# A graph network on one core: the last gathers in two buffers, output between their batches, float16 scale factors behind the output projection

## The chip, the cores and the metric

The kernel runs on one core of a Trainium2 chip. The metric is the device time of one execution in microseconds (us); the time before is the median of five runs. A profiled execution gives a trace with the time of every instruction on each engine: PE (matrix products; PEld its weight loads), DVE (vector), ACT (scalar functions), POOL (GpSimd, which here also issues the indirect DMAs) and SP (which issues the other DMAs).

## The reference

Four layers over a graph of N = 3327 nodes with 128 features and a dense 0/1 adjacency matrix `adj`. Every layer computes `x = x + layer(relu(layernorm(x)), adj)`.

```
layer 0   two rounds of swish((adj @ h) @ W + b)
layer 1   attention in 128 heads of width 8, scores + 2 * adj, softmax, then out @ Wo.T
layer 2   agg = adj @ h; msg = relu(agg @ W_msg.T + b); GRU cell of msg and h
layer 3   lap(A, x) = d * (A @ (d * x)),  d = 1 / sqrt(row sums of A)
          z = leaky_relu(lap(adj, h) @ W1 + b1)
          S = exp(-distance(z_i, z_j) / 2), only the 4 nearest of each row kept
          out = lap(S + adj, h) @ W2 + b2
```

In the last line the product with `S + adj` falls into two parts: a dense product with `adj`, and a sum over four rows per node, weighted by S. One of the four is the node itself.

## The kernel before

Nodes are laid out as 128 partitions by T = 26 tiles. Layer 0 and the projections take some 0.6 ms, the attention runs from there to about 10610 us by an order written out by hand, and everything that follows is the function `tail(general)`. There a scheduler decides at build time in which order the instructions of each engine stand; at run time each engine works through its own list in order, and semaphores connect them. `tail(False)` is what runs here; `tail(True)` is a general version in a loop that is passed zero times.

`tail` begins with the output projection of the attention (pool `lo`). For each of the 26 tiles, a load brings `o` (SP, L664), DVE normalises it (L666, L667), PE transposes it (L672), ACT copies the transposes to `oT` (L673), PE multiplies by `wo_s` into `yp` (L676) and DVE adds `yp` to `xs` (L677). Three buffers hold `o`. Pieces of tiles (0 to 3, 4 to 12, 13 to 25) go through the LayerNorm (L157 to L164) as soon as they are ready, and are split into two float16 parts (L214, L218) for the products with `adj`. The second product (L230, 26 loads of a 16-bit row block by L227) and layer 2 follow, then the layer 3 product, the distances with the four largest entries of each row (L862, L863), and the last product.

Ahead of the projection in the source stands `scales` (L586 to L625). It works out, from the largest and smallest `d1` and the norms of the columns of `w2`, the scale factors with which values are brought into float16 range: `d1_in`, `d1_out`, `into4`, `back4` and the flag `wide`. It has one small matrix product on PE (L601, into `c2`), which needs the square of `w2_s` (ACT, L598), two reductions of it (DVE, L602, L603), a square root (ACT, L605), a maximum over partitions (POOL, L595) and some dozen DVE instructions on 1 to 26 columns (L606 to L624). `d1_in` is first used behind layer 2.

Rows `y` of all nodes are written to DRAM (`yd`). While the last dense product runs, `gather(t)` collects the neighbours: for each tile of a batch three indirect DMAs on POOL (L886, 128 rows of 512 bytes each) fill `rows`; DVE multiplies by `sim` (L895, reading `rows`), adds up (L896, L897), scales (L898) and adds to `xs` (L899). L894 begins the sum of the next batch with the node's own row. There are five batches of 5, 5, 5, 5 and 6 tiles, and one buffer `rows`, so the gathers of a batch wait until L895 of the batch before has read it. When the product is done, seven PSUM accumulators are copied to `agg`, four of them by DVE (L191), three by ACT (L189). Then the output: in groups of four tiles PE transposes `agg` (L908), DVE scales it (L910) and adds `xs` (L911), and SP writes `o` to `out` with three DMAs (L914). The pool of `o` has three buffers.

Of the kernel before, what the change touches and what calls it, by code (L numbers as in the profile page):

```python
# [8 lines left out]
F32 = mybir.dt.float32  # L9
# [9 lines left out]
PSUM = bass.MemoryType.PSUM  # L19
DRAM = bass.MemoryType.DRAM  # L20

P = 128
# [23 lines left out]
def quads():  # L46
    return [(a, min(4, T - a)) for a in range(0, T, 4)]
# [7 lines left out]
def kernel(  # L55
# [65 lines left out]
    def over_t(small, t0=0, n=T):  # L121
        return small[:, t0 : t0 + n].unsqueeze(2).to_broadcast([P, n, D])
# [5 lines left out]
    def inv_sqrt(pool, src, name, scale=1.0, bias=0.0):  # L128
        r = pool.tile([P, T], F32, name=name)
        nc.scalar.activation(r, src, AF.Sqrt, bias=bias, scale=scale)  # L130
        nc.vector.reciprocal(r, r)
        return r
# [453 lines left out]
    def scales(pool, d1):  # L586

        d1_in, d1_out = (pool.tile([P, T], F32, name=name) for name in ("d1_in", "d1_out"))
        into4, back4 = (pool.tile([P, 1], F32, name=name) for name in ("into4", "back4"))

        ends = pool.tile([P, 4], F32, name="ends")
        both = pool.tile([P, 2], F32, name="both")
        nc.vector.tensor_reduce(both[:, 0:1], d1, AX.X, ALU.max)
        nc.vector.tensor_reduce(both[:, 1:2], d1, AX.X, ALU.min, negate=True)
        nc.gpsimd.partition_all_reduce(ends[:, :2], both, P, bass_isa.ReduceOp.max)  # L595
        sq = pool.tile([P, P + D], F32, name="w2_sq")
        nc.vector.memset(sq[:, :P], 1.0)
        nc.scalar.activation(sq[:, P:], w2_s, AF.Square)  # L598
        with tc.tile_pool(name="sc_ps", bufs=1, space=PSUM) as ps:
            c2 = ps.tile([P, D], F32, name="c2")  # L600
            nc.tensor.matmul(c2, sq[:, :P], sq[:, P:], start=True, stop=True)  # L601
            nc.vector.tensor_reduce(ends[:, 2:3], c2, AX.X, ALU.max)  # L602
            nc.vector.tensor_reduce(ends[:, 3:4], c2, AX.X, ALU.min, negate=True)  # L603
        top = pool.tile([P, 2], F32, name="ends_top")
        nc.scalar.activation(top[:, 1:2], ends[:, 2:3], AF.Sqrt, bias=tiny_c)  # L605
        nc.vector.tensor_copy(top[:, 0:1], ends[:, 0:1])  # L606
        low = pool.tile([P, 2], F32, name="ends_low")

        nc.vector.tensor_scalar(low[:, 0:1], ends[:, 1:2], -(2.0**5), None, op0=ALU.mult)
        nc.vector.tensor_scalar(low[:, 1:2], ends[:, 3:4], -(2.0**12), None, op0=ALU.mult)  # L610
        fit = pool.tile([P, 2], F32, name="ends_fit")
        nc.vector.tensor_tensor(fit[:, 0:1], ends[:, 0:1], low[:, 0:1], op=ALU.is_le)
        nc.vector.tensor_tensor(fit[:, 1:2], ends[:, 2:3], low[:, 1:2], op=ALU.is_le)
        nc.vector.tensor_mul(wide, fit[:, 0:1], fit[:, 1:2])
        nc.vector.tensor_scalar(wide, wide, -1.0, 1.0, op0=ALU.mult, op1=ALU.add)

        inv = pool.tile([P, 2], F32, name="ends_inv")
        nc.vector.reciprocal(inv, top)
        nc.vector.tensor_mul(into4, inv[:, 0:1], inv[:, 1:2])
        nc.vector.tensor_mul(back4, top[:, 0:1], top[:, 1:2])  # L620
        nc.vector.tensor_scalar(d1_in, d1, inv[:, 0:1], PART, op0=ALU.mult, op1=ALU.mult)
        nc.vector.tensor_scalar(d1_out, d1, top[:, 0:1], 0.5 / PART, op0=ALU.mult, op1=ALU.mult)
        nc.vector.tensor_scalar_mul(into4, into4, PART / 2)
        nc.vector.tensor_scalar_mul(back4, back4, 1.0 / PART)  # L624
        return d1_in, d1_out, into4, back4  # L625
# [4 lines left out]
    def tail(general):  # L630
# [13 lines left out]
        with ExitStack() as s:  # L644
# [4 lines left out]
                split_unless_general(parts, h, p, scale=PART)  # L649

            h, done = layernorm_relu(pool, halved)
            d1 = inv_sqrt(pool, deg, "d1")
            d1_in, d1_out = d1, d1
            if not general:
                d1_in, d1_out, into4, back4 = scales(pool, d1)
            with tc.tile_pool(name="lo", bufs=3) as lo, tc.tile_pool(name="lo_ps", bufs=2, space=PSUM) as ps:
                wo_s = lo.tile([NH, E, D], F32, name="wo_s", bufs=1)
                nc.gpsimd.dma_start(wo_s, wo)
                for t in range(T):
                    kp = rows_of(t)  # L660
                    o = lo.tile([P, EA, NH], F32, name="o")
                    src = ot.rearrange("e (p t c) -> t p e c", t=T, c=NH)[t]
                    for p0, p1 in ((0, kp),) if kp == P else ((0, 112), (112, kp)):
                        nc.sync.dma_start(o[p0:p1], src[p0:p1])  # L664
                    inv = lo.tile([P, NH], F32, name="inv")
                    nc.vector.reciprocal(inv[:kp], o[:kp, E, :])  # L666
                    nc.vector.tensor_mul(o[:kp, :E, :], o[:kp, :E, :], inv[:kp].unsqueeze(1).to_broadcast([kp, E, NH]))  # L667
                    oT = lo.tile([NH, E, P], F32, name="oT")
                    for quad in range(2):
                        tp = ps.tile([P, 4, P], F32, name="tp")  # L670
                        for j in range(4):
                            nc.tensor.transpose(tp[:, j, :kp], o[:kp, 4 * quad + j, :], ident[:kp, :kp])  # L672
                        nc.scalar.copy(oT[:, 4 * quad : 4 * quad + 4, :kp], tp[:, :, :kp])  # L673
                    yp = ps.tile([P, D], F32, name="yp")
                    for e in range(E):
                        nc.tensor.matmul(yp[:kp], oT[:, e, :kp], wo_s[:, e, :], start=(e == 0), stop=(e == E - 1))  # L676
                    nc.vector.tensor_add(xs[:kp, t, :], xs[:kp, t, :], yp[:kp])  # L677
                    done(t + 1)


            a_pool = s.enter_context(tc.tile_pool(name="adj_in", bufs=1 if general else 4))
# [190 lines left out]
                nc.vector.tensor_sub(moved[:, T - 1 :], moved[:, T - 1 :], last_row)  # L872


            cuts = list(range(0, T - T % 5, 5)) + [T]
            near_0 = 0 if general else 1

            def gather(t):
                if t not in cuts[:-1]:
                    return  # L880
                p = slice(t, cuts[cuts.index(t) + 1])
                n = p.stop - p.start
                rows = gpool.tile([P, n, 4 - near_0, D], F32, name="rows")
                for i in range(n):
                    for k in range(near_0, 4):
                        nc.gpsimd.indirect_dma_start(  # L886
                            out=rows[:, i, k - near_0, :],
                            out_offset=None,
                            in_=yd,
                            in_offset=bass.IndirectOffsetOnAxis(ap=idx[:, t + i, k : k + 1], axis=0),  # L890
                        )
                w = gpool.tile([P, n, 4, D], F32, name="w")
                if not general:
                    nc.vector.tensor_mul(w[:, :, 0], y[:, p], sim[:, p, 0:1].to_broadcast([P, n, D]))  # L894
                nc.vector.tensor_mul(w[:, :, near_0:], rows, sim[:, p, near_0:].unsqueeze(3).to_broadcast([P, n, 4 - near_0, D]))  # L895
                nc.vector.tensor_add(w[:, :, 0:2], w[:, :, 0:2], w[:, :, 2:4])  # L896
                nc.vector.tensor_add(w[:, :, 0], w[:, :, 0], w[:, :, 1])  # L897
                nc.vector.tensor_mul(w[:, :, 0], w[:, :, 0], over_t(d2_out, t, n))  # L898
                nc.vector.tensor_add(xs[:, p], xs[:, p], w[:, :, 0])  # L899

            with tc.tile_pool(name="l3_g", bufs=1) as gpool:
                agg = new_agg(pool)
                adj_product(agg, y, parts, gather)
            with tc.tile_pool(name="l3_o", bufs=3) as opool, tc.tile_pool(name="l3_ops", bufs=3, space=PSUM) as ps:
                for t0, n in quads():
                    op = ps.tile([P, 4, D], F32, name="op")
                    for j in range(n):
                        nc.tensor.transpose(op[:, j, :], slots(agg)[:, t0 + j, :], ident)  # L908
                    o = opool.tile([P, 4, D], F32, name="o")
                    nc.vector.tensor_mul(o[:, :n], op[:, :n], over_t(d2_out, t0, n))  # L910
                    nc.vector.tensor_add(o[:, :n], o[:, :n], xs[:, t0 : t0 + n, :])  # L911
                    for p0, p1, n_t in ROW_PARTS:
                        m = min(t0 + n, n_t) - t0
                        nc.sync.dma_start(dram(out, (p0 * T + t0) * D, [[T * D, p1 - p0], [D, m], [1, D]]), o[p0:p1, :m])  # L914
            if not general:
                need = pool.tile([P, 1], F32, name="need")
                nc.vector.tensor_reduce(need, moved, AX.X, ALU.max)
# [130 lines left out]
```

## Time and profile before

| | us |
|---|---|
| median of 5 runs | 11358.35 |
| lowest and highest run | 11336.96, 11369.28 |
| the profiled execution | 11340.12 |
| its span, first to last instruction | 11338.3 |

| stretch of the profile (us) | what runs |
|---|---|
| 600 to 10610 | projections and attention |
| 10611 to 10715 | output projection; PE busy 80 of 104 us |
| 10715 to 11181.7 | layers 2 and 3 up to the first gather |
| 11181.7 to 11303 | gathers; POOL busy 82.4 of 121.3 us |
| 11303 to 11338.3 | last batch, output, end of the program |

Over the whole span PE is busy 96% of the time, ACT 90%, DVE 83% and POOL 50%; these shares are those of the attention and say little about the two short stretches that the change touches. In the profile, a row gives an instruction's start and length in us; the brackets give how long its engine had been idle before it, and what ended that.

### The profile page before, as it was taken

How to read it: one execution, taken by the hardware profiler on the slowest of the kernel's cores; microseconds unless marked ns; L12 is line 12 of the kernel's file. 1: busy time of each engine (PE TensorE's matmuls, PEld its weight loads, DVE VectorE, ACT ScalarE, POOL GpSimd, SP SyncE). 2: the span in 40 equal slices, each digit the busy share in tenths (PEclk: the TensorE clock that was granted, in tenths of full speed). 3: DMA queues.
4: the chain of work that ended last, by engine and by line, in shares of the span. 5: the costliest groups of instructions: out<-in, count | busy, mean ns of one | idle time of the engine just before them, and what ended most of it. 6: DMA issues, size and time to landing. Idle time of an engine off the chain costs nothing. (4 is left out here: it accounts for less than half of the span.)

```text
span 11338.3 us, 210656 instructions
## 1 busy us (share of the span) xinstructions
PE 10935.1 (96%) x79505; PEld 3034.8 (27%) x79530; DVE 9415.2 (83%) x15475; ACT 10223.5 (90%) x9152; POOL 5711.6 (50%) x6196
## 2 busy tenths in 40 slices
PE   9789999999999999999999999999999999999896
PEld 4322222222222222222222222222222222222453
DVE  8678888888888888888888888888888888888655
ACT  0379999999999999999999999999999999999532
POOL 0135555555555555555555555555555555555203
PEclk9899999999999999999999999999999999999998
DMA  7754444444444444444444444444444443444432
GB/s 265 243 126 62 65 67 61 65 66 61 69 63 63 68 62 67 65 61 68 63 65 68 61 65 66 60 68 64 61 69 61 64 63 54 60 57 57 139 106 96
DMA packets 475903, 888.06 MB, mean 78 GB/s; under 512 B 91473, under 2 KB 422722, under 8 KB 439293
## 3 DMA queue, kind: packets, MB, share of 16 engines
q1 hardware_dynamic: 471114, 864.70, 43.7%
q8 instruction: 629, 10.31, 0.5%
q0 software_dynamic: 3760, 9.79, 0.3%
q14 instruction: 400, 3.27, 0.1%
HBM read 761.66 MB, written 112.46 MB: 77 GB/s over the span
## 5 line engine op out<-in xcount | busy, mean ns | idle before, releaser
L497 DVE TENSOR_TENSOR p<-early,a 128x476 f32<-128x476 f32 (+1 forms) x14560 | 8441.4, 646 | 1428.7 <-PE early L492 1178.5
L502 ACT ACTIVATE p<-p 128x2380 f32<-128x2380 f32 (+1 forms) x2912 | 6742.7, 2315 | 15.8 <-DVE p L497 0.4
L509 PE MATMUL acc<-p,v 128*9 128x476 f32 (+1 forms) x46592 | 5887.7, 564 | 44.6 <-POOL p L500 24.6
L500 POOL TENSOR_TENSOR p<-p,e 128x476 f32<-128x476 f32 (+1 forms) x2912 | 3538.8, 1215 | 3286.2 <-ACT p L498 3227.1
L498 ACT ACTIVATE p<-late 128x476 f32<-128x476 f32 (+1 forms) x5824 | 4513.4, 892 | 49.4 <-PE late L495 27.8
L492 PE MATMUL early<-q,k 32*128 32x476 f32 (+1 forms) x14560 | 2882.6, 477 | 18.6 <-DVE p L497 18.6
L492 PE MATMUL late<-q,k 32*128 32x476 f32 (+1 forms) x8736 | 2798.1, 478 | 62.0 <-ACT p L498 36.3
L374 POOL CAST k<-k_in 128x256 fp32r<-128x256 f32 x2912 | 1944.7, 701 | 1185.5 <-DMA q<-qt 577.0
L492 PEld LDWEIGHTS late<-q,k 32*128 32x128 f32 x8736 | 1065.4, 181 | 4765.5 <-ACT p L498 3197.4
L495 PE MATMUL late<-a,two_i 128*128 128x476 bf16 (+1 forms) x5824 | 2180.8, 374 | 0.0
L492 PEld LDWEIGHTS early<-q,k 32*128 32x128 f32 x14560 | 1144.2, 181 | 23.2 <-DVE p L497 19.3
L509 PEld LDWEIGHTS acc<-p,v 128*9 128x9 f32 x46592 | 711.4, 88 | 1424.7 <-issue 1184.5
L495 PEld LDWEIGHTS <-two_i 128*128 128x128 bf16 x5824 | 556.1, 95 | 1328.5 <-issue 1328.5
L189 ACT COPY agg<-agg_ps 128x512 f32<-128x512 f32 x15 | 8.2, 591 | 489.5 <-PE agg_ps L204 289.8
L230 PE MATMUL agg_ps<-a,part 128*128 128x512 bf16 (+1 forms) x1067 | 227.8, 370 | 8.9 <-ACT agg L861 3.2
L272 POOL TENSOR_SCALAR a<-a_in 128x476 bf16<-128x476 f32 (+2 forms) x156 | 222.0, 1423 | 0.5
L410 ACT ACTIVATE qk_st<-pp 128x1024 fp32r<-128x1024 f32 (+1 forms) x52 | 53.3, 1024 | 148.5 <-DMA qt<-qk_st 69.7
L856 PE MATMUL sp<-yT,hT 128*128 128x512 f32 (+1 forms) x364 | 170.9, 611 | 12.3 <-ACT agg L861 6.3
L272 POOL TENSOR_SCALAR a<-a 128x476 bf16<-128x476 f32 (+1 forms) x26 | 36.4, 1402 | 287.2 <-DMA a<-in_adjT_dram 287.2
L204 PE MATMUL agg_ps<-a,h 128*128 128x512 f32 (+2 forms) x364 | 147.5, 568 | 26.7 <-DVE h L164 26.7
L411 DVE SCALAR_TENSOR_TENSOR qk_st<-pp,qk_st 128x1024 fp32r<-128x1024 f32 (+1 forms) x52 | 63.7, 1224 | 122.3 <-ACT qk_st L410 122.3
L518 DVE COPY o<-acc 105x476 f32<-105x476 f32 (+1 forms) x224 | 144.4, 645 | 4.6 <-PE acc L509 4.6
(231 smaller groups left out, 2427.5 us busy)
## 6 DMA issues: line engine op xcount, KB each, us to landing
k_in<-kt SPq DMA_DIRECT2D x1792, 208.0 KB
v<-vd SPq DMA_DIRECT2D x896, 117.0 KB
a<-in_adjT_dram SPq DMA_DIRECT2D x50, 1663.5 KB
a<-adj SPq DMA_DIRECT2D x78, 831.8 KB
q<-qt SPq DMA_DIRECT2D x3072, 14.9 KB
a_in<-in_adjT_dram SPq DMA_DIRECT2D x125, 238.0 KB
qt<-qk_st SPq DMA_DIRECT2D x25, 1024.0 KB
kt<-qk_st SPq DMA_DIRECT2D x25, 1024.0 KB
```

The source lines that it names most:

```text
L204: nc.tensor.matmul(acc[c][:, :w], lhs[:kp, t, :], a[:kp, c0 : c0 + w], start=(t == 0), stop=(t == T - 1))
L230: nc.tensor.matmul(acc[c][:, :w], part[:, t, :], a[:, c0 : c0 + w], start=(t == 0 and i == 0), stop=(t == T - 1 and i == len(parts) - 1),)
L272: nc.gpsimd.tensor_scalar(a2[:kp, :w], a, 2.0, None, op0=ALU.mult)
L374: nc.gpsimd.tensor_copy(k, slots(k_in)[:, t : t + 2, :])
L492: nc.tensor.matmul(sp[:, :we], pairs[t // 2][r, t % 2, :], q4[r, :we], start=True, stop=ways[i] != "I")
L495: nc.tensor.matmul(late[:, i - n_d, :we], two_i, a2[:, :we], start=False, stop=True)
L497: nc.vector.tensor_tensor(p8[:, places[i], :we], early[i][:, :we], a2[:, :we], op=ALU.add)
L498: nc.scalar.activation(p8[:, places[n_d] : places[3] + 1, :we], late[:, :, :we], AF.Exp)
L500: nc.gpsimd.tensor_tensor(p8[:, places[3], :we], p8[:, places[3], :we], e_a[:, :we], op=ALU.mult)
L502: nc.scalar.activation(p8[:, :5, :we], p8[:, :5, :we], AF.Exp)
L509: nc.tensor.matmul(acc[32 * i : 32 * i + EA, :w], v4[:kp, i, t, :], p8[:kp, PLACES[t % 2][i], :w], start=(t == 0), stop=(t == T - 1),)
L856: nc.tensor.matmul(sp[:, c0 : c0 + w], slots(zT)[:, t, :], z2T[:, cols], start=True, stop=False)
```

## The change

Three edits, all in `tail`:

- `inv_sqrt` and `scales`, with all they compute, move in the source from ahead of the output projection to behind it.
- The last gathers are cut into six batches of 5, 5, 5, 5, 4 and 2 tiles, in two buffers: batches 0, 1, 2 and 4 use `rows0`, batches 3 and 5 use `rows1`.
- Only batches 0, 1 and 2 are given to the product as work beside it. The other three follow in the source, and the groups of the output that are complete are written between them.

Line numbers of the changed kernel: the projection is L660 (load), L662, L663, L668, L669, L672, L673; the gathers are L888, the sums L896 to L901; the output is L916 (transposes), L918, L919 and L922.

```diff
             h, done = layernorm_relu(pool, halved)
-            d1 = inv_sqrt(pool, deg, "d1")
-            d1_in, d1_out = d1, d1
-            if not general:
-                d1_in, d1_out, into4, back4 = scales(pool, d1)
             with tc.tile_pool(name="lo", bufs=3) as lo, tc.tile_pool(name="lo_ps", bufs=2, space=PSUM) as ps:
...
                     done(t + 1)
+
+            d1 = inv_sqrt(pool, deg, "d1")
+            d1_in, d1_out = d1, d1
+            if not general:
+                d1_in, d1_out, into4, back4 = scales(pool, d1)
...
-            cuts = list(range(0, T - T % 5, 5)) + [T]
+            cuts = [c for c in (0, 5, 10, 15, 20, 24) if c < T] + [T]
             near_0 = 0 if general else 1
-
-            def gather(t):
-                if t not in cuts[:-1]:
-                    return
-                p = slice(t, cuts[cuts.index(t) + 1])
+            batches = [slice(t0, t1) for t0, t1 in zip(cuts, cuts[1:])]
+
+            def gather(i):
+                p = batches[i]
                 n = p.stop - p.start
-                rows = gpool.tile([P, n, 4 - near_0, D], F32, name="rows")
+                turn = i % 2 if i > 2 else 0
+                rows = gpool.tile([P, n, 4 - near_0, D], F32, name=f"rows{turn}")
...
+            n_beside = min(3, len(batches))
             with tc.tile_pool(name="l3_g", bufs=1) as gpool:
                 agg = new_agg(pool)
-                adj_product(agg, y, parts, gather)
-            with tc.tile_pool(name="l3_o", bufs=3) as opool, tc.tile_pool(name="l3_ops", bufs=3, space=PSUM) as ps:
-                for t0, n in quads():
+                adj_product(agg, y, parts, lambda t: gather(cuts.index(t)) if t in cuts[:n_beside] else None)
+                with tc.tile_pool(name="l3_o", bufs=3) as opool, tc.tile_pool(name="l3_ops", bufs=3, space=PSUM) as ps:
+                    to_write = quads()
+                    for i in range(n_beside - 1, len(batches)):
+                        if i >= n_beside:
+                            gather(i)
+                        while to_write and sum(to_write[0]) <= batches[i].stop:
+                            t0, n = to_write.pop(0)
...
```

The body that writes one group of the output is the same as before, indented further.

More of the change, by code (lines that the diff above doesn't have):

```diff
@@ L872, in tail @@
                 nc.vector.tensor_sub(moved[:, T - 1 :], moved[:, T - 1 :], last_row)
-            cuts = list(range(0, T - T % 5, 5)) + [T]
+            cuts = [c for c in (0, 5, 10, 15, 20, 24) if c < T] + [T]
             near_0 = 0 if general else 1
-            def gather(t):
-                if t not in cuts[:-1]:
-                    return
-                p = slice(t, cuts[cuts.index(t) + 1])
+            batches = [slice(t0, t1) for t0, t1 in zip(cuts, cuts[1:])]
+            def gather(i):
+                p = batches[i]
                 n = p.stop - p.start
-                rows = gpool.tile([P, n, 4 - near_0, D], F32, name="rows")
-                for i in range(n):
+                turn = i % 2 if i > 2 else 0
+                rows = gpool.tile([P, n, 4 - near_0, D], F32, name=f"rows{turn}")
+                for j in range(n):
                     for k in range(near_0, 4):
                         nc.gpsimd.indirect_dma_start(
-                            out=rows[:, i, k - near_0, :],
+                            out=rows[:, j, k - near_0, :],
                             out_offset=None,
                             in_=yd,
-                            in_offset=bass.IndirectOffsetOnAxis(ap=idx[:, t + i, k : k + 1], axis=0),
+                            in_offset=bass.IndirectOffsetOnAxis(ap=idx[:, p.start + j, k : k + 1], axis=0),
                         )
@@ L897, in gather @@
                 nc.vector.tensor_add(w[:, :, 0], w[:, :, 0], w[:, :, 1])
-                nc.vector.tensor_mul(w[:, :, 0], w[:, :, 0], over_t(d2_out, t, n))
+                nc.vector.tensor_mul(w[:, :, 0], w[:, :, 0], over_t(d2_out, p.start, n))
                 nc.vector.tensor_add(xs[:, p], xs[:, p], w[:, :, 0])
+            n_beside = min(3, len(batches))
             with tc.tile_pool(name="l3_g", bufs=1) as gpool:
                 agg = new_agg(pool)
-                adj_product(agg, y, parts, gather)
@@ L904, in tail @@
-            with tc.tile_pool(name="l3_o", bufs=3) as opool, tc.tile_pool(name="l3_ops", bufs=3, space=PSUM) as ps:
-                for t0, n in quads():
[L906 to L914, printed above, removed]
+                adj_product(agg, y, parts, lambda t: gather(cuts.index(t)) if t in cuts[:n_beside] else None)
@@ new lines, in tail @@
+                with tc.tile_pool(name="l3_o", bufs=3) as opool, tc.tile_pool(name="l3_ops", bufs=3, space=PSUM) as ps:
[5 more added lines that the diff above has]
+                            t0, n = to_write.pop(0)
+                            op = ps.tile([P, 4, D], F32, name="op")
+                            for j in range(n):
+                                nc.tensor.transpose(op[:, j, :], slots(agg)[:, t0 + j, :], ident)
+                            o = opool.tile([P, 4, D], F32, name="o")
+                            nc.vector.tensor_mul(o[:, :n], op[:, :n], over_t(d2_out, t0, n))
+                            nc.vector.tensor_add(o[:, :n], o[:, :n], xs[:, t0 : t0 + n, :])
+                            for p0, p1, n_t in ROW_PARTS:
+                                m = min(t0 + n, n_t) - t0
+                                nc.sync.dma_start(dram(out, (p0 * T + t0) * D, [[T * D, p1 - p0], [D, m], [1, D]]), o[p0:p1, :m])
```

## The prediction

> **What bounds the kernel now.** I read the page first: the chain that ended last names the gathers (POOL L886), the products on gathered rows (DVE L895 to L898) and the output. The attention stage is untouched, so I cut the rest into stretches with the view by windows (columns: stretch, length, busy PE, PEld, DVE, ACT, POOL, granted clock, DMA share, GB/s), then asked for the tile `rows` and the timelines.
>
> ```profile
> 11181.70:11303.00 121.30, 57.65 (x270) 27.02 (x274) 27.93 (x24) 1.56 (x3) 82.42 (x78) 0.76 0.47 163
> L886 POOL DMA_INDIRECT rows<-yd,idx x78: 943/947/2078, 11181.7 to 11302.1; - x78
>   DVE w L895: 16.6, 4
> ```
>
> From 11181.7 to 11303.0 POOL issues 78 gathers back to back; PE ends the third product at 11243, sixty us earlier. The last line lists POOL's own idle time: four waits, 16.6 us together, for L895 to free the one buffer `rows`. POOL's timeline round the first wait, and DVE's beside it (start, length, instruction, idle before):
>
> ```profile
> 11199.49 0.95 POOL L886 DMA_INDIRECT rows<-yd,idx  x1 [0.30 <-issue]
> 11204.63 2.08 POOL L886 DMA_INDIRECT rows<-yd,idx  x1 [4.19 <-DVE w L895]
> 11207.01 1.41 POOL L886 DMA_INDIRECT rows<-yd,idx  x1 [0.30 <-issue]
> 11208.73 1.42 POOL L886 DMA_INDIRECT rows<-yd,idx  x1 [0.30 <-issue]
> ...
> 11202.20 2.16 DVE L895 TENSOR_TENSOR w<-rows,sim 128x1920 f32<-128x1920 f32 x1 [25.69 <-DMA rows<-yd,idx]
> 11204.39 1.49 DVE L896 TENSOR_TENSOR w<-w 128x1280 f32<-128x1280 f32 x1
> 11205.92 0.82 DVE L897 TENSOR_TENSOR w<-w 128x640 f32<-128x640 f32 x1
> 11206.78 0.82 DVE L898 TENSOR_TENSOR w<-w,d_out 128x640 f32<-128x640 f32 x1
> ```
>
> A gather step is 0.95 + 0.30 = 1.25 us. The last gather of a batch ends at 11200.44, lands 1.76 later, L895 takes 2.16 and POOL starts 0.27 after that: 4.19 idle instead of 0.30. The next three gathers are also stretched, by 1.13 + 0.46 + 0.47 = 2.06 us. Their ends fit one reading: 0.13 into a gather POOL needs what a running DVE TENSOR_TENSOR holds, waits for that instruction's end, and then takes 0.82 (L896 ends 11205.88, + 0.82 = 11206.70; the gather ended 11206.71).
>
> The stage adds up: 78 steps 97.4, four waits at 3.85 over the usual gap 15.4, four stretches 8.3; sum 121.1, measured 121.3.
>
> After the last landing DVE still has to work; and in the output projection PE starts late:
>
> ```profile
> 11304.74 2.56 DVE L895 TENSOR_TENSOR w<-rows,sim 128x2304 f32<-128x2304 f32 x1 [21.30 <-DMA rows<-yd,idx]
> 11312.41 0.42 DVE L191 COPY agg<-agg_ps 128x255 f32<-128x255 f32 x1
> ...
> 10617.97 1.23 DVE L667 TENSOR_TENSOR o<-o,inv 128x1024 f32<-128x1024 f32 x1
> 10623.06 0.95 DVE L666 RECIPROCAL inv<-o 128x128 f32<-128x128 f32 x1 [0.45 <-DMA o<-ot]
> ...
> 10621.29 0.80 PE L601 MATMUL c<-w_sq 128*128 128x128 f32 x2 [12.06 <-ACT w_sq L598]
> 10622.71 1.94 PE L672 MATMUL tp<-ident,o 128*128 128x128 f32 x8 [0.63 <-PE c L601]
> 10627.12 1.04 PE L672 MATMUL tp<-ident,o 128*128 128x128 f32 x8
> ```
>
> Tile 0 is normalised at 10619.20, but L601 stands ahead of its transposes and waits for `w2` (ACT L598, 10620.92); PE begins at 10622.71 and then runs almost without a gap, 3.22 us a tile, to 10710.6.
>
> **The change, part by part.** The built program's order is known without a run. POOL issues 15 gathers of batch 0, 9 of batch 3, 15 of batch 1, 6 of batch 3, 15 of batch 2, 12 of batch 4, 6 of batch 5. So batch 3, in the second buffer, fills the first two waits.
>
> *Waits.* A wait lasts until 4.2 us after the batch's last gather. Batch 3's nine gathers cover 11 us, its six 7.5: both waits go. Batch 4 stands straight behind batch 2 and shares its buffer: this wait stays. Batch 5 needs L897 of batch 3, about 9 us after batch 2 landed, while batch 4's twelve gathers take 15: no wait. Three of four go: 3 × 3.85 = **-11.5**.
>
> *Stretching.* The L897 that POOL used to sit out now runs beside gathers, and behind batch 4's issue lies the DVE work of batches 2 and 3 together. TENSOR_TENSOR work beside gathers grows from 19.3 us to 31.1 (durations of L894 to L899, by size). Replaying "wait for the running DVE instruction" with a landing of 1.7 gives the starts of before to 0.3 us, and for the new order 2.1 + 2.2 + 5.4 + 0.7 = 10.4 in place of 8.3: **+2.1**. No such row exists for L897 beside gathers, so the bounds are wide: 0 in all (gathers unaffected, -8.3) and 31.1 (POOL stands through all DVE work, +22.8). I take the replay; it fits twelve stretched gathers.
>
> Here the Trainium skill can be weighed. SBUF — State Buffer, section Who interferes with whom, says that a DVE instruction with two SBUF inputs blocks a GpSimd instruction that reads SBUF until it ends, but infers that tensor_tensor does not hold up descriptor generation. The 2.08 us gather agrees with the first and speaks against the second; by the second the sum would be that of the first rival.
>
> *The end.* Batch 5 has two tiles instead of six. DVE from landing to the last copy of `agg` was 11304.74 to 11312.83, 8.09 us. Now: L897 0.99, L898 0.73, L899 and L900 0.46 each, L901 0.33 until the copies, these 0.6 × 3 + 0.42: 5.2. **-2.9** (bounds -4 to 0). The output is *not* moved forward, though the source puts it between the batches: the four DVE copies (L191) stand behind the last batch's L901 in DVE's order, and PE's transposes need all of them. ACT's copies were done at 11243.7 before too. In the output DVE issues L918 twice ahead of the first L919, so the first store leaves 0.45 us later, and a three-buffer chain of stores carries that to the end: **+0.45** (0 to +0.7).
>
> *The factors.* No DMA moves with them. On ACT, L605 goes behind the last copy L673; the square L598 stays ahead of the first, so that copy cannot start before 10621.23. On PE, tile 0's transposes start at about 10619.4 (were 10622.71), its products at 10621.9 (were 10624.5). Then tile 1 becomes late: its load lands at 10623.06 as before, and 0.95 + 1.23 later, at 10625.4, PE may start; it started at 10627.12. **-1.7** (0 if later loads set the pace, -2.6 if only ACT does). The loads of tiles 3 and 4, issued as buffers come free, land 4.1 us after issue, over 2 us before PE needs them. DVE's L606, behind POOL's all-reduce (10628.5), comes after tile 3 is normalised, so a late result has some 4 us of cover.
>
> At the other end L601, L602 and L603 now lie between the projection and the second product: 2.9 us after the last `yp`, then four transposes, 0.66. The product waits anyway for its first load, 10710.65 to 10715.0, 4.3 us. Cover 0.7 us; without it up to 1 us comes back. Some dozen DVE instructions of 0.1 to 0.3 us enter the last LayerNorm piece; its tiles 13 to 25 are needed 13 × 2.95 = 38 us into the product, so they cost nothing. All later stages shift with PE.
>
> Sum: -11.5 + 2.1 - 2.9 + 0.45 - 1.7 = **-13.5 us**. The profiled execution took 11340.12 (span 11338.3), so 11326.6; the median of the five runs is 18.2 higher, 11358.35, so **11344.8**.
>
> **Rivals.** *Gathers are not stretched at all*, because what lengthened them was the restart after a wait and not DVE: 97.4 + 3.85 = 101.3 in place of 121.1, with the rest -24 us, 11334. For it: all twelve stretched gathers follow a wait. Against it: their ends fit DVE's to 0.01 us. Chance 0.08. The skill's inference, above, would have it so.
>
> *POOL stands still through every run of DVE work:* 97.4 + 3.85 + 31.1 = 132.3, +11.2 in the stage, **+7 us** in all, 11365, slower than before. It decides from the point where POOL loses 0.77 of the overlapped DVE time (31.1 × 0.77 = 8.3 + 11.5 + 4.1); before, it lost 0.43, and gathers slipped in between instructions. Chance 0.07.
>
> *The projection does not start earlier in effect* (loads pace it, or L603 holds PE at the product): -11.8, 11346.5. For it: eighteen of L666's starts waited for a load. Against it: PE's gaps in that loop are 0.3 us. Chance 0.17.
>
> **Numbers.** The forecast has 0.68. 0.2%, about what a measurement of this kernel can tell from no change, is 22.7 us, so -13.5 lies within it. The five runs lie from 21.4 below to 10.9 above their median; I let a median of such runs be off by 8 (an estimate from that spread). Range: 11334 less 8, 11326, up to 11362, which leaves out half of the slow rival. Faster by over 0.2%: most of the first rival, and the forecast with a lucky median, 0.18. Slower by over 0.2%: 0.05, the slow rival with an unlucky median. Within: 0.77.
>
> **What would show it.** Gather stage 111.7 us long; one POOL wait of about 4 us in it, ahead of batch 4's twelve gathers; the gather under L897 stretched by 1 to 2 us, two or three of batch 4 over 1.2; L191 after the last L901; first L668 transposes near 10619.4 and the second product near 10713.3. Wrong: gathers at 0.95 beside L897 (first rival), a POOL idle of 7 us per batch (second), transposes of the second product waiting for L603 (third), or a store of `out` before the last gather.

## The result, and the profile after

Median after: 11344.15 us (34 runs), beside 11354.47 us for the kernel before (58 runs): ratio 0.999, 95% interval [0.9985, 0.9994]. The forecast was 11344.8. That the two medians lie within 0.7 us is in part luck: the median before, over more runs, came 3.9 us below the 11358.35 that the forecast started from, and the change itself is -10.3 us where -13.5 was forecast. The profiled execution took 11324.42 us (span 11322.7) against 11340.12: 15.7 us less, of which 3.7 lie in the attention, which no edit touches. All places in the two traces are therefore compared from the start of the attention's last copy, L518 (10609.32 before, 10605.66 after).

The view by windows of the changed kernel, over the gathers, then the tile `rows` (columns as in the prediction):

```profile
11180.57:11291.39 110.82, 66.80 (x248) 25.21 (x252) 31.32 (x28) 0.00 (x0) 83.60 (x78) 0.69 0.53 178
L888 POOL DMA_INDIRECT rows<-yd,idx x78: 940/944/2222, 11180.6 to 11290.4; - x78
...
  DVE w L897: 4.1, 1
```

The stage is 110.8 us instead of 121.3, and one wait for L897 is left of four. POOL's timeline round the place of the first wait and at the one that is left, then DVE's:

```profile
11202.03 2.00 POOL L888 DMA_INDIRECT rows<-yd,idx  x1 [0.30 <-issue]
11204.33 1.22 POOL L888 DMA_INDIRECT rows<-yd,idx  x1 [0.30 <-issue]
11205.86 1.41 POOL L888 DMA_INDIRECT rows<-yd,idx  x1 [0.30 <-issue]
11207.57 1.41 POOL L888 DMA_INDIRECT rows<-yd,idx  x1 [0.30 <-issue]
...
11263.94 2.07 POOL L888 DMA_INDIRECT rows<-yd,idx  x1 [4.06 <-DVE w L897]
```

```profile
11201.05 2.16 DVE L897 TENSOR_TENSOR w<-rows,sim 128x1920 f32<-128x1920 f32 x1 [25.77 <-DMA rows<-yd,idx]
11203.24 1.49 DVE L898 TENSOR_TENSOR w<-w 128x1280 f32<-128x1280 f32 x1
...
11293.12 0.95 DVE L897 TENSOR_TENSOR w<-rows,sim 128x768 f32<-128x768 f32 x1
...
11295.75 0.43 DVE L901 TENSOR_TENSOR xs<-xs,w 128x256 f32<-128x256 f32 x1
11296.09 2.21 DVE L191 COPY agg<-agg_ps 128x512 f32<-128x512 f32 x4
```

Where POOL used to stand for 4.19 us it now stands 0.30, and the gather beside L897 takes 2.00: L897 ends at 11203.21, the gather 0.82 later. At the end, DVE needs 5.2 us from the landing to the last copy (11293.12 to 11298.30) instead of 8.1, and L191 stands behind the last L901. PE at the projection and ahead of the second product:

```profile
10615.57 1.94 PE L668 MATMUL tp<-ident,o 128*128 128x128 f32 x8 [10.00 <-DVE o L663]
10621.77 1.06 PE L668 MATMUL tp<-ident,o 128*128 128x128 f32 x8
...
10709.27 0.63 PE L694 MATMUL tp<-ident,h 128*128 128x128 f32 x4 [2.00 <-DVE ends L603]
```

From L518, tile 0's transposes start at 9.9 (13.4 before) and tile 1's at 16.1 (17.8). The second product starts at 105.5 (105.7 before).

What nobody had forecast is in the third product (L230). PE's waits, the view by windows, and rows of PE's timeline:

```profile
PE agg_ps L230 <- issue: 43.0, 29, 3.6
11200.50:11260.00 59.50, 21.15 (x40) 4.14 (x41) 13.90 (x12) 0.00 (x0) 46.00 (x44) 0.51 0.31 92
```

```profile
11225.28 0.38 PE L230 MATMUL agg_ps<-a,part 128*128 128x255 bf16 x1 [0.83 <-issue]
11228.77 0.58 PE L230 MATMUL agg_ps<-a,part 128*128 128x512 bf16 x1 [3.10 <-issue]
11230.89 0.59 PE L230 MATMUL agg_ps<-a,part 128*128 128x512 bf16 x1 [1.54 <-issue]
11232.99 0.58 PE L230 MATMUL agg_ps<-a,part 128*128 128x512 bf16 x1 [1.52 <-issue]
...
11264.52 8.67 PE L230 MATMUL agg_ps<-a,part 128*128 128x512 bf16 x28 [3.12 <-issue]
```

From 11200.5 to 11264, PE issues its products mostly one at a time, 1.4 to 4.2 us apart, with nothing that the profile shows to wait for: 40 products and 41 weight loads are recorded in the 59.5 us up to 11260, where it did 120 products in the 24.8 us up to 11199.5. The granted clock is 0.51 there. The starts lie multiples of some 0.70 us apart (3.49, 2.12, 2.10). Full speed comes back at 11264.52, 0.6 us behind POOL's one pause (11259.88 to 11263.94). The product, which ended at 11243 in the kernel before, now ends at 11296.12, just as the last L901 does (11296.18), and the copies L191 follow L901 without an idle time. So the delay cost nothing here, by 0.1 us; what it hangs on is what most of the experiments ask.

### The profile page after: what moved, and what is told of

It is laid out like the page before. It is cut to its first block, busy times and chain, and to the rows that moved or that the text cites. A ratio compares the mean times of both kernels' runs of the same rounds, so it can differ in the third digit from the quotient of the medians.

```text
span 11322.7 us, 210647 instructions
## 1 busy us (share of the span) xinstructions
PE 10952.2 (97%) x79505; PEld 3037.1 (27%) x79530; DVE 9416.2 (83%) x15481; ACT 10219.5 (90%) x9152; POOL 5708.3 (50%) x6196
## 3 DMA queue, kind: packets, MB, share of 16 engines
q8 instruction: 629, 10.31, 0.5%
## 5 line engine op out<-in xcount | busy, mean ns | idle before, releaser
L498 ACT ACTIVATE p<-late 128x476 f32<-128x476 f32 (+1 forms) x5824 | 4513.6, 892 | 49.0 <-PE late L495 25.5
L230 PE MATMUL agg_ps<-a,part 128*128 128x512 bf16 (+1 forms) x1067 | 243.5, 380 | 50.0 <-issue 43.4
L230 PEld LDWEIGHTS <-part 128*128 128x128 f16 x1092 | 109.6, 101 | 178.8 <-issue 78.2
```

Source lines behind the costliest of these rows:

```text
L230: nc.tensor.matmul(acc[c][:, :w], part[:, t, :], a[:, c0 : c0 + w], start=(t == 0 and i == 0), stop=(t == T - 1 and i == len(parts) - 1),)
L498: nc.scalar.activation(p8[:, places[n_d] : places[3] + 1, :we], late[:, :, :we], AF.Exp)
```

## The experiments

The runs came in three batches, each on one chip with the kernel before beside it: e1 to e4 on chip B, e5 to e8 on chip C, the last four on chip D. Ratios go by the kernel before on the same chip.

### e1: the factors alone

```diff
(kernel before)
-            d1 = inv_sqrt(pool, deg, "d1") ... scales(pool, d1)   # ahead of the projection
+            d1 = inv_sqrt(pool, deg, "d1") ... scales(pool, d1)   # behind it
```

> The kernel before with the factors moved behind the projection and nothing else. Theory of the prediction: tile 0's transposes start 3.3 us earlier against the last product of the attention (L518), tile 1's load then bounds, and from there all is 1.7 us earlier, up to the first gather (572.4 us after L518 in before, so 570.7). Rival (clock): PE stands idle about 3 us around L603 just ahead of the second product, its granted clock falls to 0.5 there, and the first 28 products take over 8 us; then the second product starts 0 to 0.5 us earlier and the first gather comes 0.5 to 2.5 us later than in before. The median can't tell these apart (both within 3 us of before); the places in the trace can.

Measured: 11328.27 us against 11331.24, ratio 0.9997 [0.9988, 1.0007]. The timeline of PE at the projection:

```profile
10600.35 1.94 PE L668 MATMUL tp<-ident,o 128*128 128x128 f32 x8 [10.03 <-DVE o L663]
...
10606.63 1.04 PE L668 MATMUL tp<-ident,o 128*128 128x128 f32 x8
```

From L518 (10590.42) these are 9.93 and 16.21: 3.5 and 1.6 us earlier than before, as forecast. The second product starts at 105.09 (105.70 before), the first gather comes at 571.69 (572.41): 0.7 us earlier. The clock rival falls: in the first 5 us of the second product the granted clock was 0.69 here and 0.66 to 0.72 in the eleven later runs; only the profile of the changed kernel had 0.50. Over all profiles, the first gather comes 571.7 to 574.9 us after L518 with the factors behind the projection (twelve profiles, mean 573.1), and 572.4 and 573.7 with them ahead (before, e2). So the 1.7 us are seen at the projection, but not at the second product (0.6) and not at the gathers (where they go is said below); the spread there, 3 us, is larger than the term.

### e2: the gathers and the output alone

```diff
(changed kernel)
+            d1 = inv_sqrt(pool, deg, "d1") ... scales(pool, d1)   # back ahead of the projection
-            d1 = inv_sqrt(pool, deg, "d1") ... scales(pool, d1)   # behind it
```

> The changed kernel with the factors back in their old place: two buffers and the new output loop alone. Theory: all of the gain is here: gather stage 110 to 112 us (before 121.3), end 4 us shorter, time 12 to 15 us below before. Rival (the factors matter): time 5 us or more above that of the changed kernel. Theory on PE: its third product again stops running at speed about 20 us after the first gather and recovers only in POOL's one pause, ending within 1 us of the last L901.

Measured: 11313.94 us, 17.3 below before, ratio 0.9986 [0.9977, 0.9995]; stage 110.32 us, first gather to the end of the last. This part alone has a gain of the changed kernel's size, and e1 has none that is clear of the noise. PE is slow again, from 18.4 us after the first gather to 11248.7, just behind POOL's one pause (11243.6 to 11247.6); the product ends at 11280.1, the copies of `agg` begin at 11279.33.

### e3: no wait at all

```diff
-                turn = i % 2 if i > 2 else 0
+                turn = (0, 0, 0, 1, 2, 1)[i]
```

> The changed kernel with a third buffer for batch 4, so that POOL never waits for DVE: 78 gathers without a pause. Theory S (supply): while POOL issues gathers without a pause, PE gets its instructions one at a time, from about 20 us after the first gather until the gathers end; the stage is 106 to 108 us (110.8 in the changed kernel), but some 125 products are still open at its end, 29 us of PE work, so that the product ends 20 to 25 us later than in the changed kernel and the time is 15 to 22 us above the changed kernel's, 5 to 10 us above before. Rival A (only the recording slows PE, the timed runs don't show it): time 3 to 4 us below the changed kernel's. Rival B (PE's slow stretch has to do with its own place in the product, not with the gathers): product ends where it did, time 0 to 4 us below the changed kernel's.

Measured: 11332.08 us, ratio 1.0 [0.9991, 1.0009]: 18 us above e2 on the same chip (the changed kernel itself was not timed on it; e2 differs from it by the factors alone), though the stage is shorter, 107.36 us, and the tile `rows` has no wait for DVE. PE's timeline, at the end of the gathers (last end 11264.29):

```profile
11260.14 0.59 PE L230 MATMUL agg_ps<-a,part 128*128 128x512 bf16 x1 [0.83 <-issue]
11262.23 0.58 PE L230 MATMUL agg_ps<-a,part 128*128 128x512 bf16 x1 [1.50 <-issue]
11264.32 29.56 PE L230 MATMUL agg_ps<-a,part 128*128 128x512 bf16 x130 [1.50 <-issue]
```

PE does single products as long as POOL gathers, and 130 in one run from the moment POOL stops. Now the product is the bound. The loss is in the median of the timed runs too, so that rival A (an effect of the recording) falls, and with it rival B (the gathers have nothing to do with it): the last wait, which a reader of the POOL rows alone would take away next, was worth more than it cost.

### e4: a pause without DVE

```diff
+                if i == 0 and not general:
+                    with tc.issue_after(last.ins):
+                        nc.gpsimd.tensor_add(spare, spare, spare)   # 128x1792, behind the first 15 gathers
...
```

`last` is the gather issued last. The lines that set up and fill the buffer `spare` are not shown.

> The changed kernel with one POOL instruction of its own (an addition on 128x1792 float32, about 4 us, on a buffer that nobody else uses) behind the first 15 gathers; no wait for DVE in it. Theory S: PE recovers in this pause as it did in the kernel before, so the next slow stretch starts about 20 us after POOL's gathers start again; the product ends 25 us or more earlier than in the changed kernel, the gather stage is 4 to 8 us longer, and so is the time. Rival B: PE runs slow from the same moment to the same moment as in the changed kernel, whatever POOL does at 20 us. Rival C (PE recovers by DVE's work or by what POOL waits for, not by the pause in the gathers): no recovery in the pause itself.

Measured: 11317.31 us, ratio 0.9988 [0.9979, 0.9997]. POOL's timeline round the addition, and PE's rows at the turns:

```profile
11178.65 0.95 POOL L891 DMA_INDIRECT rows<-yd,idx  x1 [0.30 <-issue]
11186.40 3.29 POOL L899 TENSOR_TENSOR spare<-spare 128x1792 f32<-128x1792 f32 x1 [6.80 <-issue]
11189.87 1.56 POOL L891 DMA_INDIRECT rows<-yd,idx  x1 [0.18 <-issue]
```

```profile
11180.00 0.38 PE L230 MATMUL agg_ps<-a,part 128*128 128x512 bf16 x1 [0.27 <-issue]
11182.10 2.75 PE L230 MATMUL agg_ps<-a,part 128*128 128x512 bf16 x13 [1.73 <-issue]
...
11208.66 0.38 PE L230 MATMUL agg_ps<-a,part 128*128 128x512 bf16 x1 [0.35 <-issue]
...
11278.75 4.55 PE L230 MATMUL agg_ps<-a,part 128*128 128x512 bf16 x13 [1.51 <-issue]
```

The gathers stop for 10 us. PE had just begun to do single products (one at 11180.0, then 1.73 us of idle time); from 11182.10, 2.5 us after the last gather's end, it runs on at speed. It turns slow again 18.8 us after the gathers start again, until 3.1 us after they end (11275.68). Rivals B and C fall: PE is at speed again while the gathers pause, where in the changed kernel it was slow, and POOL waits for nothing of DVE's there (DVE's work alone doesn't help: in the changed kernel PE stays slow through it). My expectation that the product ends 25 us earlier was wrong: with this addition POOL's order changed and its later pause was gone, so the product ended 122 us after the first gather instead of 115.5.

### e5 and e6: smaller gathers, less DVE work

```diff
e5
-                            out=rows[:, j, k - near_0, :],
+                            out=rows[:64, j, k - near_0, :],
...
e6
-                nc.vector.tensor_add(w[:, :, 0:2], w[:, :, 0:2], w[:, :, 2:4])
-                nc.vector.tensor_add(w[:, :, 0], w[:, :, 0], w[:, :, 1])
-                nc.vector.tensor_mul(w[:, :, 0], w[:, :, 0], over_t(d2_out, p.start, n))
-                nc.vector.tensor_add(xs[:, p], xs[:, p], w[:, :, 0])
+                nc.vector.tensor_add(xs[:, p], xs[:, p], w[:, :, 3])
```

> The changed kernel with gathers of 64 rows instead of 128 (partitions 64 to 127 are left out of the gathers and of the products on gathered rows). Theory S says that PE slows some 15 gathers after POOL starts without a pause; this run asks what is counted. If it is rows moved (15 x 128 = 1920 of them), PE slows after some 30 gathers. If it is gathers, after some 15, whatever they take. If it is time, after 19 us, which is 15 gathers if a step still takes 1.25 us and more if it is shorter.

> The changed kernel without the sums of the gathered rows: L898, L899 and L900 are left out, one addition of 128x640 into xs stays. Theory of the prediction (a gather waits for the end of the TENSOR_TENSOR that DVE is running): the gathers' lengthening beyond 0.95 falls from 9.75 us to 5 to 6, the gather stage from 110.8 to about 106.6; every stretched gather ends 0.82 us after a DVE instruction's end. Rival (what stretches gathers is the restart or the landing rows, not DVE's work): lengthening stays near 9.75, stage 110 to 111. PE's slow stretch should be there as in the changed kernel.

e5 (timed once, 11308.0 us): PE never slowed; the product ended 55.3 us after the first gather. Whether rows, gathers or time are counted stays open, since no kernel slowed on this chip (below). A gather of 64 rows takes 0.90 us at the median, one of 128 takes 0.94.

e6 (timed once, 11303.79 us): POOL's and DVE's timelines behind the first batch:

```profile
11187.25 2.01 POOL L888 DMA_INDIRECT rows<-yd,idx  x1 [0.30 <-issue]
11189.56 1.41 POOL L888 DMA_INDIRECT rows<-yd,idx  x1 [0.30 <-issue]
11191.28 0.94 POOL L888 DMA_INDIRECT rows<-yd,idx  x1 [0.30 <-issue]
```

```profile
11186.28 2.16 DVE L897 TENSOR_TENSOR w<-rows,sim 128x1920 f32<-128x1920 f32 x1 [28.07 <-DMA rows<-yd,idx]
11188.48 0.82 DVE L898 TENSOR_TENSOR xs<-xs,w 128x640 f32<-128x640 f32 x1
11189.33 0.82 DVE L896 TENSOR_TENSOR w<-y,sim 128x640 f32<-128x640 f32 x1
```

The first stretched gather ends 0.82 us after L897 (11188.44 + 0.82 = 11189.26), the second 0.82 us after L896 (11190.15 + 0.82 = 11190.97). With three DVE instructions left of six, two gathers are stretched instead of four. All lengthening beyond 0.95 sums to 6.1 us (9.7 in the changed kernel), the stage to 107.2: DVE's work is what lengthens gathers. PE's slow stretch, which I had expected here too, did not come.

### e7 and e8: the output really early, with and without pauses

```diff
-                        if i >= n_beside:
-                            gather(i)
+                        if i >= n_beside:
+                            with tc.issue_after(ends_of["gathers"].ins), tc.issue_after(ends_of["output"].ins):   # e7
+                            with tc.issue_after(ends_of["output"].ins):                                           # e8
+                                gather(i)
```

`ends_of` holds the last gather issued and the last L922 (the addition that ends a group of the output); the lines that fill it are not shown.

> The changed kernel with two orders forced: POOL issues batch 3 behind batch 2 (so the waits of 4 us ahead of batches 1 and 2 are back, and the one ahead of batch 4 goes), and DVE's work of batch 3 and later stands behind the copies of agg and the output of the tiles before. Theory S: with a pause every 19 us PE runs the third product at speed and ends it 62 us after the first gather (115.5 in the changed kernel); the copies and most of the output then lie beside the gathers, and only the last quad's output is left behind the last batch: 18 us from the last gather to the end instead of 31.3. Stage 115.5 to 120 us (two waits 7.7, stretches 10 to 14). Time 4 to 9 us below the changed kernel's, 14 to 24 below before. Rival (PE's slow stretch is not undone by these waits): the product ends late, DVE's later batches wait for it, and the time is 10 us or more above the changed kernel's.

> As e7, but POOL's order is left as in the changed kernel (batch 3 fills the first two waits): the early output alone. Theory S: PE is slow from 20 us after the first gather until the one pause ahead of batch 4, so the product still ends 115 us after the first gather; DVE's batch 3 now stands behind it, and POOL's batch 5 waits for batch 3's buffer. End some 11 us later than in the changed kernel, about level with before (-5 to +5). Rival (the early output helps by itself, PE's speed is not what matters): time 10 us or more below the changed kernel's.

Measured on chip C: e7 11319.05 us, 22.5 below before, 0.9981 [0.9972, 0.999]; e8 11312.56 us, 29.0 below, 0.9979 [0.9969, 0.9988]. e7 did as expected (stage 116.5, end 18.5 us after the last gather), e8 did not. Its third product on PE's timeline, and the view by windows over 30.9 us of it in which POOL issued 24 gathers (PE is the first engine):

```profile
11151.53 74.53 PE L230 MATMUL agg_ps<-a,part 128*128 128x512 bf16 x364 [3.19 <-ACT agg L862]
```

```profile
11195.17:11226.07 30.90, 30.89 (x155) 14.87 (x152) 6.95 (x7) 0.94 (x2) 23.89 (x24) 1.00 0.80 284
```

364 products in one run at clock 1.00, without any pause of POOL, with POOL's order that of the changed kernel. Theory S as I had put it (unbroken gathers slow PE) was wrong: something else has to be there. All slow profiles had come from other chips than these four; the last batch put both kinds on one chip.

### The last four, on one chip

The kernels are the changed kernel, e3, e7 and e8 without further edits.

> The changed kernel itself once more, beside e3, e7 and e8 on one chip. So far PE's slow stretch was there in the profiles of the changed kernel, e2, e3 and e4 and not in those of e5 to e8, but the kernels with it and those without it ran on different chips. Theory C: whether PE slows is a matter of the chip (or of how the program lies in it), so that here either all of the kernels without early pauses (this one, e3, e8) show it or none does. Theory K: it is a matter of the kernel: this one and e3 show it, e8 doesn't. In both the time of this kernel is the same, 8 to 17 us below before, since the copies of agg stand behind the last batch anyway.

> e3 (no POOL wait at all) again, on the same chip as the changed kernel. With the slow stretch (theory K, or theory C on a chip that has it): product ends after the gathers, time 12 to 22 us above the changed kernel's, as before in e3. Theory C on a chip without it: product ends about 62 us after the first gather, time 2 to 5 us below the changed kernel's (one wait less).

> e7 (POOL's waits of batches 1 and 2 kept, output early) again. In theory C this is the kernel that doesn't mind the chip: with its pauses PE slows for 1 to 3 us at most, the product ends 62 to 65 us after the first gather, the time is 6 to 10 us below the changed kernel's on either kind of chip.

> e8 (early output, POOL's order as in the changed kernel) again. Theory K, or theory C on a chip without the slow stretch: 12 to 15 us below the changed kernel's, the product ended about 55 to 62 us after the first gather. Theory C on a chip with it: the product ends 115 us after the first gather and the time is 5 to 15 us above the changed kernel's.

Measured (before: 11339.13 us); the product's end is counted from the first gather:

| kernel | median us | against before, ratio | product's end |
|---|---|---|---|
| changed kernel | 11323.80 | -15.3, 0.9987 [0.9979, 0.9996] | 116.7 |
| e3, no wait | 11344.81 | +5.7, 1.0004 [0.9995, 1.0013] | 138.9 |
| e7, two early pauses | 11313.64 | -25.5, 0.998 [0.9972, 0.9989] | 63.3 |
| e8, early output, no early pause | 11348.01 | +8.9, 1.0009 [1.0, 1.0017] | 120.7 |

K falls, and C fits: on chip D the three kernels without early pauses are all slow. e8, the same program, was 29.0 us below before on C and 8.9 above it here. What it cost stands in POOL's timeline: batch 5 waits for L899 of batch 3, which stands behind the copies of `agg`:

```profile
11296.17 0.94 POOL L890 DMA_INDIRECT rows<-yd,idx  x1 [29.85 <-DVE w L899]
```

e7 on the same chip, PE's timeline round the first pause, and POOL's:

```profile
11186.32 0.38 PE L230 MATMUL agg_ps<-a,part 128*128 128x512 bf16 x1 [0.45 <-issue]
11187.71 0.38 PE L230 MATMUL agg_ps<-a,part 128*128 128x512 bf16 x1 [1.01 <-issue]
11189.14 23.25 PE L230 MATMUL agg_ps<-a,part 128*128 128x512 bf16 x105 [1.05 <-issue]
```

```profile
11185.45 0.94 POOL L890 DMA_INDIRECT rows<-yd,idx  x1 [0.30 <-issue]
11190.51 2.07 POOL L890 DMA_INDIRECT rows<-yd,idx  x1 [4.12 <-DVE w L899]
```

PE had just turned slow (11185.6) when the wait came, and the wait set it right. e7 is 10.2 us below the changed kernel here. The two intervals overlap, but the profiles agree: from the first gather to the end of the span e7 takes 135.1 us on C and 135.3 on D, the changed kernel 142.1 and 143.1. It is the version to keep: its median lay 22.5 and 25.5 us below before on the two chips, while e8's hangs on the chip.

## Why the prediction was right, and what it missed

**Waits.** Three of four went: 15.4 us over the usual gap became 3.8, so -11.6; forecast -11.5.

**Stretching.** Lengthening beyond 0.95 rose from 8.3 to 9.7 us, +1.4; forecast +2.1. The ends fit the replay (2.00 beside L897; batch 4's run 2.07, 1.42, 1.42, 1.76), and e6 shows the cause. The sizes fit less well than their sum: the four runs of stretched gathers have 2.2, 2.2, 3.9 and 1.3, where the replay had 2.1, 2.2, 5.4 and 0.7. The first rival (no stretching) is refuted, as is the second (POOL stands through all DVE work): 31.3 us of DVE work lay beside the gathers and cost 9.7. The stage, 111.7 forecast, was 110.8.

**The end.** DVE from landing to the last copy: 5.2 us, forecast 5.2. The output was not moved forward, as read from the built order; e7 shows what moving it is worth. The term of the output was mis-sized: +0.45 was forecast, and from the last gather's end to the span's end everything together took 31.3 us instead of 35.3, so -4.0, of which the output has -1.1. One row of it: the output's transposes, 24 in 5.36 us before, went 20 in 2.88. PE came to them 2.3 us after a product instead of 70 us. The traces of e5 and e6, where the product ended early, show what that did: PE had stood 59.6 and 57.1 us, and the first ten transposes come 0.21 us apart at a granted clock of 0.50, as before; in the changed kernel they come 0.12 us apart at 1.00. From the first transpose to the span's end it takes 24.8 and 25.0 us in e5 and e6, 24.2 in the changed kernel and 25.3 before. So some 0.6 of the -1.1 came with the late product and was luck; e1, with the output as before, also took 24.8, so that the rest lies within the spread.

**The factors.** The step named held: the load of tile 1 sets the pace, and tile 1's transposes start 1.7 us earlier. The lead is still 1.7 us at tile 17, which starts 70.4 us after L518 (72.1 before). Then "all later stages shift with PE" failed, and not at the place that the third rival names. In both kernels PE stands 2.6 to 2.7 us for "issue" ahead of tile 17, a gap that the prediction overlooked when it put PE's gaps in that loop at 0.3 us (before, then the changed kernel):

```profile
10681.43 1.07 PE L672 MATMUL tp<-ident,o 128*128 128x128 f32 x8 [2.69 <-issue]
...
10676.06 1.84 PE L668 MATMUL tp<-ident,o 128*128 128x128 f32 x8 [2.63 <-issue]
```

Behind it the granted clock was 1.00 before and 0.62 in the changed kernel, so that the tile took 4.46 us instead of 3.25, which eats 1.2 us of the lead. In the twelve other profiles too, e2 with the factors ahead among them, this tile takes 4.4 to 4.6 us: the profile of before is the exception, and the loss is not the change's doing. L603 held the second product's transposes for 2.0 us, the sign that had been set down for the third rival, but PE then still stood 1.23 us for the product's first load, so the hold itself cost next to nothing. The second product started 0.2 us earlier instead of 1.7, and the first gather came 2.5 us later in the changed kernel's profile, 0.7 earlier in e1, and level over all profiles. The third rival (no earlier in effect, -11.8) can't be told from the forecast by the time.

In the profile, then: -3.7 in the attention, +2.5 up to the first gather, -10.5 in the stage, -4.0 behind it, sum -15.7. The median moved by 10.3 us in one comparison and 15.3 in the other, with -13.5 forecast: less than 0.2% either way.

**Missed.** I took the third product as ended "at 11243, sixty us earlier" and gave it no term. The row of before that could have warned was there: PE stands 1.13 us for "issue" ahead of a product at 11202.34, just behind the first batch's gathers (which end at 11200.44), and runs on at speed from 11203.06, in POOL's pause:

```profile
11202.34 0.38 PE L230 MATMUL agg_ps<-a,part 128*128 128x512 bf16 x1 [1.13 <-issue]
11203.06 23.80 PE L230 MATMUL agg_ps<-a,part 128*128 128x512 bf16 x107 [0.34 <-issue]
```

The terms of the gathers and of the end were right by their mechanism. That the sum held as well was luck: DVE's copies stand behind the last batch, so that 53 us of delay fitted into the gap, with 0.1 us left. With the copies ahead of that, as in e8 on D, or with the last pause gone, as in e3, the same delay took the whole gain: e8 lay 8.9 us above before, e3 0.8 and 5.7.

## What to carry to other kernels

Before a wait is removed, ask who lives on it: here the pauses of POOL were what a product on another engine needed, and the version that removes all of them loses 21 us against the one that keeps one. Two stretches that seem sixty microseconds apart are a resource only as long as nothing slows the earlier one; look for small unexplained idle times of "issue" at the place where the pause will go. Compare variants on one chip: e8 lay 29.0 us below before on one and 8.9 above it on another.

## What the runs showed of the hardware

**PE slows beside unbroken gathers, in three of four batches of runs.** In seven profiles it is there at length (changed kernel twice, e2, e3 twice, e4, e8 on D); in three more (before, e1, e7 on D) it begins and a wait of POOL's ends it after one to three products. It begins 17 to 20 us after the first gather, 14 to 16 gathers, and ends around the next pause (from 2.5 us behind the last gather in e4 to 1.1 us behind the pause in e2) or within some 3 us of the last gather; a pause of 4 us was enough each time. Behind a pause it came again after 18.8 us (e4) and 13.7 (e8 on D), but not in the changed kernel's last 27 us, 18 gathers. It was there in the first comparison, on B and on D, not on C; but the four kernels profiled on C are not those of B, and only e7 and e8 ran on C and D both. Whether the chip itself or the way a program lies in it decides was not tried, nor what is counted. The cause stays open: the Trainium skill (Runtime: NRT & Kernel Launch, section Instruction fetch mechanics) says that instructions come in blocks of 16 KiB over a DMA queue, a cost that is mostly hidden. The trace fits the blocks: the 629 packets of the instruction queue q8 moved 10.31 MB, 16.4 KB each, and between two of them PE has 127 products recorded in 25 us in e8 on C, and 132 in 86 us in the changed kernel. So the next block was called for after about the same work, however long that took; what held PE inside a block, no view shows.

**Which DVE work lengthens a gather.** In e7 on chip D, outputs run beside gathers. DVE's and POOL's timelines:

```profile
11246.99 1.49 DVE L921 TENSOR_TENSOR o<-op,d_out 128x512 f32<-128x512 f32 x2 [1.34 <-PE op L919]
11248.40 1.28 DVE L922 TENSOR_TENSOR o<-o,xs 128x512 f32<-128x512 f32 x2
```

```profile
11247.53 0.94 POOL L890 DMA_INDIRECT rows<-yd,idx  x1 [0.30 <-issue]
11248.78 1.12 POOL L890 DMA_INDIRECT rows<-yd,idx  x1 [0.30 <-issue]
```

The gather beside L921, which reads `op` from PSUM, takes its 0.94; the one beside L922, both inputs in SBUF, takes 1.12. The Trainium skill (SBUF — State Buffer, section Who interferes with whom) draws the same line at two SBUF inputs, and this row agrees; its inference that tensor_tensor leaves descriptor generation alone is what the stretched gathers of every run here speak against.
